# Layer 2 attention in units of four heads, with the first batch's units placed among the first layer's segments

## The chip, the cores and the metric

The kernel runs on one core of one Trainium2 chip. The metric is the device time of one execution in microseconds, as the median of several runs. All times below come from the runs and from one profiled execution of the kernel before.

## The reference

The input x has 4 batches of 2048 tokens with 256 features, in float32. Two layers follow each other, each of the form x = x + s * silu(g), where s is an attention and g a feed-forward network, both on a layer norm of x.

```python
# layer 1
xn = layernorm(x)
s = dilated_attention(xn)   # 16 heads of 16; segments of 512 queries, every 8th key: 64 keys;
                            # maximum over blocks of 64 queries; then @ Wout.T
g = xn_rounded_to_fp8 @ w8.T + bias
x = x + s * silu(g)
# layer 2
xn = layernorm(x)
q, k, v = xn @ wq + bq, xn @ wk + bk, xn @ wv + bv      # rotary positions on q and k
att = softmax(causal(q @ k.T / 4))                      # 16 heads of 16, 2048 x 2048 each
s = (att @ v) @ wo + bo
g = mixture_of_experts(xn)  # 8 experts, top 2 of a softmax, capacity 2048 slots each,
                            # relu(x @ w1 + b1) @ w2 + b2, hidden 1024
x = x + s * silu(g)
```

The two parts of layer 2 that cost most are the causal attention (4 batches x 16 heads, head size 16) and the experts (16384 slots in blocks of 512).

## The kernel before, in words

Everything is float32. The order of the instructions on TensorE (PE), VectorE (DVE), ScalarE (ACT) and GpSimd (POOL) is the order of the program: the blocks under `manual_schedule` leave nothing to a scheduler. Transfers are issued from the queue of SyncE (SP), indirect ones from POOL's.

**First layer** (L133 to L380). 16 segments of 512 tokens run in a software pipeline of 8 steps per segment. `segment` writes functions into a plan by step (`at`, L175), and the plan is then run in order of steps. A segment loads x (L182), normalizes it, transposes it (`turn_x`, L199), rounds to fp8 (`to_fp8`, L213), projects q, k and v, makes scores against 64 keys (`scores0`, L273), takes block maxima and exponentials (`weigh`, L285), multiplies with the values (`values`, L297), transposes (`turn_y`), projects (`outputs`, L320), gates (`gate`), stores x1, normalizes again, and stores this norm to DRAM as `xn_d` together with the router's logits (`route`, L350). In PSUM two pair tiles of two banks each (`sc`, L52) and four tiles of one bank (`mm`, L53) are used. Most SBUF tiles have two buffers, x six, the weights w nine.

**Routing** (L398 to L552). When all segments are done, softmax, top 2 and the places in the experts' slots are computed, mostly on DVE. This is one block with nothing beside it.

**Second layer.** PSUM is divided anew: three pair tiles `sp` (L562) and two single tiles `so` (L563). For each batch, two phases follow each other in the loop L1059 to L1076:

- `maxima` (L691). For each query block qb of 512, each row group r of 128 queries and each group g of four heads, scores of 128 queries against up to 512 keys are made by four matmuls that work on 32 rows of the array each (`scores`, L677). DVE reduces full key blocks straight from PSUM (L720). The diagonal block is copied by ACT (L723), masked on POOL (L731) and reduced (L740). The negated maxima are transposed (`spread`, L751) and written as an extra row into q, so that later scores come out with the maximum subtracted.
- `attend` (L765). For each qb, g and tile kt of 128 keys, the transposed scores are made, ACT takes exponentials from PSUM (L826), POOL masks the diagonal (L831), and two items later the values are multiplied (L846). Per qb and g the result is copied (L852), transposed and divided (`heads_out`, L803), and per qb projected (`out_rows`, L771).

Beside these run side generators, which `along` (L1034) advances by costs written by hand. `project` (L594) makes q, k and v of a batch from `xn_d`; its results stay in a ring of five SBUF blocks. `experts` (L878) runs two experts' blocks beside each batch's maxima. `finish` (L956) combines the experts' outputs with s and x1 beside the last batch's `attend`. So at any time maxima (DVE) or exponentials (ACT) run, not both.

Of the kernel before, what the change touches and what calls it, by code (L numbers as in the profile page):

```python
# [18 lines left out]
P = 128  # L19
# [24 lines left out]
def d2_kernel(ctx: ExitStack, tc: tile.TileContext, t: dict):  # L44
# [6 lines left out]
    first = ExitStack()  # L51
    ps_sc = first.enter_context(tc.tile_pool(name="ps_sc", bufs=2, space=PSUM))  # L52
    ps_mm = first.enter_context(tc.tile_pool(name="ps_mm", bufs=4, space=PSUM))  # L53

    def sc_tile():
        return ps_sc.tile([P, 2, 512], F32, tag="sc", name="sc")

    def mm_tile():
        return ps_mm.tile([P, 512], F32, tag="mm", name="mm")
# [6 lines left out]
    xn_d = dram.tile([B * M + 1, D], F32, tag="xn_d", name="xn_d")  # L66
    s_d = dram.tile([B * M, D], F32, tag="s_d", name="s_d")
# [7 lines left out]
    def rows(d, n):  # L75
# [11 lines left out]
    early = ExitStack()  # L87
    logits = early.enter_context(tc.tile_pool(name="early", bufs=1)).tile(
        [P, NT, E], F32, tag="logits", name="logits"
    )  # L90
# [28 lines left out]
    def transpose2(out, in_):  # L119

        tp = mm_tile()
        for c in range(2):
            nc.tensor.transpose(tp[:, c * P : (c + 1) * P], in_[:, c * P : (c + 1) * P], ident)
        nc.scalar.copy(out, tp[:, : 2 * P].rearrange("p (c t) -> p c t", c=2))

    def silu(pool, zh):

        th = pool.tile([P, D], F32, tag="se", name="se")
        nc.scalar.activation(th, zh, AF.Tanh)
        nc.vector.scalar_tensor_tensor(zh, th, 1.0, zh, ALU.add, ALU.mult)  # L130


    with ExitStack() as l0:  # L133
        w0 = l0.enter_context(tc.tile_pool(name="w0", bufs=1))
        p2 = l0.enter_context(tc.tile_pool(name="l0p2", bufs=2))
        small = l0.enter_context(tc.tile_pool(name="l0small", bufs=4))
# [27 lines left out]
        for i in range(3):  # L164
            v_ = w0.tile([P, 8, 2, HD + 1], F32, tag=f"vbd{i}", name=f"vbd{i}")
            nc.vector.tensor_copy(v_[:, :, :, HD], bc(dmask[:, None, :], [P, 8, 2]))
            vbds.append(v_)
# [7 lines left out]
        def at(step, f, *args):  # L175
            plan.setdefault(step, []).append((f, args))

        def segment(g):
# [3 lines left out]
            def load():  # L182
                v["x"] = x = p2.tile([P, SPT, D], F32, tag="x", name="x", bufs=6)
                nc.sync.dma_start(out=x, in_=rows(x_d, g))
# [7 lines left out]
            def norm(tag):  # L192
                v[tag] = xn = p2.tile([P, SPT, D], F32, tag=tag, name=tag)
# [5 lines left out]
            def turn_x(c):  # L199
                if c == 0:  # L200
                    v["xnT"] = p2.tile([P, 2, SEG], F32, tag="xnT", name="xnT")

                    v["xdil"] = p2.tile([P, 2, 2, KN], F32, tag="xdil", name="xdil")
                tp = mm_tile()
                for a in range(SPT):
                    nc.tensor.transpose(
                        tp[:, a * P : (a + 1) * P], v["xn"][:, a, c * P : (c + 1) * P], ident
                    )
                nc.scalar.copy(v["xnT"][:, c, :], tp)
                for u in range(2):  # L210
                    nc.gpsimd.tensor_copy(v["xdil"][:, c, u, :], v["xnT"][:, c, ::DIL])

            def to_fp8(half):  # L213


                if half == 0:
                    v["xq"] = xq = p2.tile([P, 2, SEG], F32, tag="xq", name="xq", bufs=3)
# [4 lines left out]
                mag = p2.tile([P, 2, SEG], F32, tag="mag", name="mag")  # L222
# [7 lines left out]
            def q_proj(ec):  # L230
                if ec == 0:
                    v["qT"] = p2.tile([P, 2, SEG], F32, tag="qT", name="qT")
                pq = mm_tile()
                for c in range(2):
                    nc.tensor.matmul(  # L235
# [897 lines left out]
```

## Time and profile before

| | us |
|---|---|
| median of 3 runs | 4508.95 (4506.05 to 4519.44) |
| profiled execution | 4471.85 |
| its span, first to last instruction | 4470.1 |
| PE busy | 4090.9 |
| DVE busy | 2447.8 |
| ACT busy | 1664.1 |
| POOL busy | 851.3 |

The span is some 1.75 us shorter than the profiled execution's own time, and that execution was 0.8% faster than the median of the runs. A page of the profile gives busy time by engine, a division of the span in 40 slices (each 112 us), the chain of work that ended last, and groups of instructions by line. In the groups the name before `<-` is the tile written, the names after it are those read. A float32 matmul shows as two instructions, a transpose as one. "Busy" of PE includes time in which a matmul only waits in the array's pipeline or runs at a lower granted clock.

In this span the first layer takes the first 620 us, the routing about 100, and then each batch some 450 us of maxima with experts and some 450 us of exponentials. The first batch's maxima take longer (756 to 1333 us), and the last batch's exponentials, with the final combination, 394.

### The profile page before, as it was taken

Reading aid. Unit: us, or ns where it says so; the run is one execution under the profiler, and the core shown is the slowest. Engines: PE = TensorE matmul, PEld = TensorE weight load, DVE = VectorE, ACT = ScalarE, POOL = GpSimd, SP = SyncE. Lnnn points to the kernel's source line nnn. Section 1 sums busy time; section 2 is a strip of 40 time slices with the busy share of each in tenths; the row PEclk is TensorE's granted clock in tenths of the full one; section 3 lists DMA queues with packets and bytes.
Section 4 is the critical chain, followed back from the end, with each engine's and each line's share of the span. In section 5 each row is a group of like instructions: output and inputs, shape, how many; then the busy total and the mean of one; then the engine's idle time right before and its main releaser. Section 6 shows DMA issues by size and latency. Waiting matters only on the chain.

```text
span 4470.1 us, 57281 instructions
## 1 busy us (share of the span) xinstructions
PE 4090.9 (92%) x23560; PEld 1930.8 (43%) x23560; DVE 2447.8 (55%) x3622; ACT 1664.1 (37%) x2548; POOL 851.3 (19%) x1067
## 2 busy tenths in 40 slices
PE   7898966789999998899999998999999989999998
PEld 4666654344443333444433334444333344443333
DVE  7777777667761122777812226777312257775334
ACT  2333310111116664222156652211566522114775
POOL 3333323101100012111100012110000121112444
PEclk8888777699999998899999998999999989999999
DMA  2111000000100001001000001010000010102422
GB/s 77 43 43 43 29 33 25 10 15 24 38 20 6 10 6 41 20 20 39 15 10 6 10 14 46 16 40 18 6 10 6 15 36 20 39 20 74 128 94 75
DMA packets 111240, 138.48 MB, mean 31 GB/s; under 512 B 11393, under 2 KB 99842, under 8 KB 110978
## 3 DMA queue, kind: packets, MB, share of 16 engines
q1 hardware_dynamic: 95922, 98.22, 6.7%
q0 software_dynamic: 12288, 33.57, 2.4%
q8 instruction: 185, 3.03, 0.3%
q10 hardware_dynamic: 2768, 3.02, 0.2%
q14 instruction: 77, 0.63, 0.0%
HBM read 86.03 MB, written 48.24 MB: 30 GB/s over the span
## 4 chain that ended last, share of the span: by engine, by line
PE 79%; DVE 15%; issue 2%; DMA 1%; ACT 1%; POOL 1%; POOLq 0%; ACTq 0%; SPq 0%; DVEq 0%
PE sp L683 29%; PE so L846 11%; PE so L926 10%; PE so L941 9%; DVE mp L720 4%; PE so L626 3%; PE mm L300 2%; PE so L666 2%; PE mm L323 1%; PE so L635 1%; PE so L787 1%; PE sc L278 1%; DVE at_row L538 1%; PE mm L328 1%; PE mm L235 1%
## 5 line engine op out<-in xcount | busy, mean ns | idle before, releaser
L826 ACT ACTIVATE pt<-sp 128x1024 f32<-128x1024 f32 (+3 forms) x1280 | 1076.8, 893 | 577.2 <-PE sp L683 541.6
L720 DVE TENSOR_REDUCE mp<-sp 128x2 f32<-128x1024 f32 x768 | 904.5, 1220 | 317.7 <-PE sp L683 314.9
L683 PE MATMUL sp<-kT,qT 32*128 32x512 f32 (+3 forms) x5120 | 785.1, 615 | 63.9 <-DVE mp L725 25.9
L683 PE MATMUL sp<-qT,kT 32*128 32x512 f32 (+3 forms) x5120 | 783.4, 583 | 13.6 <-ACT pt L826 13.5
L846 PE MATMUL so<-pt,va 128*32 128x512 f32 (+3 forms) x5120 | 604.6, 545 | 10.9 <-POOL pt L831 10.9
L723 ACT COPY dg<-sp 128x256 f32<-128x256 f32 x512 | 165.3, 375 | 962.6 <-PE sp L683 899.1
L926 PE MATMUL so<-xTe,w 128*128 128x512 f32 x1024 | 515.9, 628 | 4.3 <-ACT xTe L918 2.0
L941 PE MATMUL so<-w,hT 128*128 128x256 f32 x2048 | 506.6, 392 | 0.3 <-DVE ot L947 0.3
L731 POOL TENSOR_SCALAR_AFFINE_SELECT dg<-dg 128x512 f32<-128x512 f32 x256 | 163.2, 640 | 1578.7 <-ACT dg L723 1578.6
L683 PEld LDWEIGHTS sp<-kT,qT 32*128 32x128 f32 x5120 | 270.6, 197 | 444.6 <-issue 146.0
L683 PEld LDWEIGHTS sp<-qT,kT 32*128 32x128 f32 x5120 | 282.9, 184 | 407.6 <-issue 254.0
L941 PEld LDWEIGHTS so<-w,hT 128*128 128x128 f32 x2048 | 374.0, 191 | 193.2 <-issue 143.5
L831 POOL TENSOR_SCALAR_AFFINE_SELECT pt<-pt 128x512 f32<-128x512 f32 x256 | 171.7, 672 | 1310.4 <-PE sp L683 677.1
L930 ACT ACTIVATE hT<-so,b 128x512 f32<-128x512 f32 x256 | 176.0, 687 | 572.5 <-PE so L926 572.5
L725 DVE TENSOR_REDUCE mp<-sp 128x2 f32<-128x256 f32 (+2 forms) x384 | 247.5, 687 | 145.2 <-ACT dg L723 144.2
L926 PEld LDWEIGHTS so<-xTe,w 128*128 128x128 f32 x1024 | 178.1, 193 | 283.1 <-issue 199.6
L846 PEld LDWEIGHTS so<-pt,va 128*32 128x32 f32 x5120 | 101.5, 108 | 418.9 <-issue 345.0
L852 DVE COPY avs<-so 128x512 f32<-128x512 f32 x64 | 44.2, 691 | 360.7 <-PE so L846 360.7
L740 DVE TENSOR_REDUCE mp<-dg 128x8 f32<-128x1024 f32 x128 | 155.0, 1211 | 31.5 <-POOL dg L731 31.5
L626 PE MATMUL so<-wqk,xT 128*128 128x512 f32 x256 | 139.9, 672 | 23.8 <-DVE xT L622 9.5
L294 ACT ACTIVATE w<-w 128x1024 f32<-128x1024 f32 x64 | 67.7, 1057 | 241.4 <-DVE w L290 241.4
L300 PE MATMUL mm<-vbd,w 128*128 128x34 f32 x1024 | 128.7, 283 | 21.5 <-DVE vbd L267 21.5
(165 smaller groups left out, 3514.9 us busy)
## 6 DMA issues: line engine op xcount, KB each, us to landing
w<-in_w_dram SPq DMA_DIRECT2D x16, 1024.0 KB, 6.3
eout<-ot SPq DMA_DIRECT2D x32, 512.0 KB, 2.9
x<-in_x_dram SPq DMA_DIRECT2D x16, 512.0 KB, 5.9
x_d<-x SPq DMA_DIRECT2D x16, 512.0 KB, 2.9
xn_d<-x1n SPq DMA_DIRECT2D x16, 512.0 KB, 3.2
xn<-xn_d SPq DMA_DIRECT2D x16, 512.0 KB
fx<-x_d SPq DMA_DIRECT2D x16, 512.0 KB, 5.5
out_dram<-fz SPq DMA_DIRECT2D x16, 512.0 KB, 4.1
```

The costliest lines, as they stand in the source:

```text
L300: nc.tensor.matmul(av[:, j * 34 : (j + 1) * 34], lhsT=v["w", j // 2][:, j % 2, a * P : (a + 1) * P], rhs=vbds[g % 3][:, j, :, :].rearrange ...
L626: nc.tensor.matmul(pqk, lhsT=xT[:, c, :], rhs=wqk[:, c, :], start=(c == 0), stop=(c == 1))
L683: nc.tensor.matmul(pairs[j // 2][:, j % 2, :w], lhsT=lhsT[r0 : r0 + 32], rhs=rhs[r0 : r0 + 32], start=True, stop=True,)
L720: nc.vector.tensor_reduce(mp[:, h0 : h0 + 2, kc], sp, AX.X, ALU.max)
L723: nc.scalar.copy(dg[:, d0 : d0 + 2, :], sp[:, :, r * P : w])
L725: nc.vector.tensor_reduce(mp[:, h0 : h0 + 2, qb + 1], sp[:, :, : r * P], AX.X, ALU.max)
L826: nc.scalar.activation(pt[:, 2 * p : 2 * p + 2, c0:], sp[:, :, : SEG - c0], AF.Exp, scale=SCALE)
L831: nc.gpsimd.affine_select(out=pt[:, :, c0 : c0 + P], in_=pt[:, :, c0 : c0 + P], compare_op=ALU.is_ge, fill=0.0, base=0, pattern=[[0, 4], [ ...
L846: nc.tensor.matmul(av[32 * j : 32 * j + 32, c0:], lhsT=va[:, kt % 4, h0 : h0 + 32], rhs=pt[:, j, c0:], start=(kt == 0), stop=last,)
L926: nc.tensor.matmul(ph, lhsT=w1[:, c, hc * P : (hc + 1) * P], rhs=xT[:, c, :], start=(c == 0), stop=(c == 1),)
L930: nc.scalar.activation(hT[:, hc, :], ph, AF.Relu, bias=b1[:, hc : hc + 1])
L941: nc.tensor.matmul(po[:, u * D : (u + 1) * D], lhsT=hT[:, hc, a * P : (a + 1) * P], rhs=w2[:, hc, :], start=(hc == 0), stop=(hc == 7),)
```

## The change

The second layer's attention is cut into 16 units: unit n is the group g = n % 4 of four heads of batch n // 4. The pieces of the change:

- PSUM is divided once for the whole program: three pair tiles `sp`, one bank `av` for the value sums, and one bank `mm` for everything else. The first layer uses the same pair tiles for its transposes, q, scores, values and outputs, and `mm` for the rest. Its SBUF pool has one buffer for most tiles (x four, w six, two sets of values).
- `project` reads the transposed norm, which the first layer now stores to DRAM too (`xT_ds`), so it makes no transposes of x. It writes q, k and v to DRAM. `load_unit` loads q, k and v of a unit into a set of SBUF tiles. There is one set during the first layer, two afterwards.
- `maxima(n)` and `attend(n)` work on a unit. The values are multiplied one item after their exponentials (two before). Heads are stored to DRAM (`y_ds`); `out_project` reads them back and projects.
- `attention` yields the order: while there is one set, maxima of a unit, then its exponentials, then the next unit. With two sets, each item of `attend(n)` is followed by one step of `maxima(n + 1)`, three items late.
- The first layer is a generator, and so is the routing. During the first layer, from 30% of its hand-written cost on, `project` and then the units of the first batch (`EARLY = 4`) are advanced. Routing, all experts and the final combination run beside the paired units. In the experts' second product each tile of 128 slots has its own bank use (two shared one before).

```diff
-    first = ExitStack()
-    ps_sc = first.enter_context(tc.tile_pool(name="ps_sc", bufs=2, space=PSUM))
-    ps_mm = first.enter_context(tc.tile_pool(name="ps_mm", bufs=4, space=PSUM))
+    ps_s = ctx.enter_context(tc.tile_pool(name="ps_s", bufs=3, space=PSUM))
+    ps_v = ctx.enter_context(tc.tile_pool(name="ps_v", bufs=1, space=PSUM))
+    ps_m = ctx.enter_context(tc.tile_pool(name="ps_m", bufs=1, space=PSUM))
...
+    def load_unit(n):
+        b, g = n // 4, n % 4
+        held[n] = sets[(sets.index(held[n - 1]) + 1) % len(sets) if n else 0]
+        qT, kT, va = held[n]
+        nc.sync.dma_start(out=qT, in_=q_ds[b][g])
+        nc.sync.dma_start(out=kT, in_=k_ds[b][g])
+        nc.sync.dma_start(
+            out=va[:, :, :VW],
+            in_=v_ds[b][:, g * VW : (g + 1) * VW].rearrange("(i p) c -> p i c", p=P),
+        )
...
+        yield from start(0)
+        for _ in maxima(0):
+            yield MX_T, 1
+            turn()
+        for n in range(NU):
+            two = len(sets) == 2 and n + 1 < NU
+            if two:
+                yield from start(n + 1)
+            a = attend(n)
+            m = maxima(n + 1) if two else iter(())
+            a_on, step = True, 0
+            while True:
+                if a_on:
+                    a_on = next(a, None) is not None
+                    if a_on:
+                        yield S_T, 0
+                        next(a)
+                m_on = step < LEAD or next(m, None) is not None
+                if not (a_on or (two and m_on)):
+                    break
+                yield (AV_T if a_on else 0.0) + (MX_T if two and step >= LEAD else 0.0), 1
+                turn()
+                step += 1
+            units_done[0] += 1
+            if not two and n + 1 < NU:
+                yield from start(n + 1)
+                for _ in maxima(n + 1):
+                    yield MX_T, 1
+                    turn()
...
+        with ExitStack() as l0:
+            went = 0.0
+            for cost in first_layer(l0):
+                went += cost
+                if EARLY:
+                    f = max(0.0, (went / L0_T - 0.3) / 0.7)
+                    if f:
+                        prj.until(prj_share())
+                    while f and 0 in ready and not att.over and att.went < f * EARLY * UNIT_T:
+                        if units_done[0] == EARLY - 1 and 1 not in ready:
+                            prj.step()
+                            break
+                        att_step([])
+                elif went / L0_T > 0.35:
+                    prj.until(PRJ_T * min(1.0, (went / L0_T - 0.35) / 0.55))
+        ub = ctx.enter_context(tc.tile_pool(name="ub", bufs=1))
+        sets.append(unit_set(ub, "b"))
+        done = {}
+        opr = Side(out_project(ub, done))
+        with ExitStack() as rt:
+            rou = Side(routing(rt))
+            t0 = att.went
+            while not rou.over:
+                rou.burst = 3
+                att_step([
+                    (prj, 0, prj_share), (opr, 0, lambda: 1e9),
+                    (rou, 0, lambda: (att.went - t0) * 2.2), (rou, 1, lambda: (att.went - t0) * 2.2),
+                ])
+        with ExitStack() as xs:
+            ep = xs.enter_context(tc.tile_pool(name="ex", bufs=2))
+            exp = Side(experts(ep, 0, E), 2)
+            exp.step()
+            t0 = att.went
+            last = 13.7 * UNIT_T
+            while not exp.over:
+                att_step([
+                    (prj, 0, prj_share), (opr, 0, lambda: 1e9),
+                    (exp, 1, lambda: EXP_T * (att.went - t0 - 2.0) / (last - t0)),
+                ])
+        fp = ctx.enter_context(tc.tile_pool(name="fp", bufs=2))
+        fin = Side(finish(fp, done))
+        t0 = att.went
+        while not att.over:
+            att_step([
+                (opr, 0, lambda: 1e9),
+                (fin, 1, lambda: NT * (att.went - t0) / (16 * UNIT_T - t0)),
+                (fin, 0, lambda: NT * (att.went - t0) / (16 * UNIT_T - t0)),
+            ])
```

A `Side` runs one step of its generator per call of `until` (experts two, routing three) as long as its cost is below the share given. `att_step` advances the attention by one yield; kind 0 stands between scores and values, kind 1 after the maxima's scores, and kind 2 means that the unit's batch has not been projected yet. `prj_share` is PRJ_T x (1.2 + att.went / (4 UNIT_T)), UNIT_T is 120, L0_T 443.

## The prediction

> **What bounds the kernel now.** I read the page's parts 1, 2 and 4 first: who is busy, when, and on which chain.
>
> ```profile
> PE 4090.9 (92%) x23560; PEld 1930.8 (43%) x23560; DVE 2447.8 (55%) x3622; ACT 1664.1 (37%) x2548; POOL 851.3 (19%) x1067
> ...
> PE   7898966789999998899999998999999989999998
> DVE  7777777667761122777812226777312257775334
> ACT  2333310111116664222156652211566522114775
> PEclk8888777699999998899999998999999989999999
> ...
> PE 79%; DVE 15%; issue 2%; DMA 1%; ACT 1%; POOL 1%; POOLq 0%; ACTq 0%; SPq 0%; DVEq 0%
> ```
>
> TensorE is busy for 92% and carries 79% of the chain that ended last. DVE and ACT alternate: where the maxima run DVE is at 7 or 8 tenths and ACT at 1 or 2; where the exponentials run it is the other way round. The granted clock is 0.8 in the first layer, 0.6 after it, 1.0 later. Next, sums by stage (columns: window, its length, busy us of PE, PEld, DVE, ACT, POOL, clock, DMA):
>
> ```profile
> 20.00:620.00 600.00, 526.31 (x2742) 394.15 (x2741) 446.87 (x1009) 186.82 (x397) 220.17 (x251) 0.82 0.12 39
> 620.00:721.00 101.00, 46.17 (x268) 38.18 (x268) 91.36 (x176) 1.99 (x4) 37.19 (x27) 0.79 0.05 13
> ...
> 850.00:880.00 30.00, 24.69 (x86) 10.40 (x88) 18.78 (x24) 3.82 (x11) 3.18 (x5) 0.50 0.00 0
> ...
> 1790.00:2240.00 450.00, 434.00 (x2074) 205.94 (x2071) 341.17 (x366) 88.52 (x191) 62.84 (x84) 0.97 0.07 23
> 2240.00:2700.00 460.00, 429.74 (x3056) 158.68 (x3054) 104.65 (x192) 275.55 (x339) 50.35 (x76) 0.97 0.05 16
> 4076.00:4470.00 394.00, 366.34 (x2721) 123.33 (x2720) 146.84 (x241) 282.65 (x336) 172.71 (x192) 0.98 0.33 104
> ```
>
> 20 to 620 is the first layer (16 segments, 36.4 us each by the spacing of its repeated rows), 620 to 721 the routing, 1790 to 2240 maxima with experts, 2240 to 2700 exponentials, 4076 to 4470 exponentials with the final combination. 850 to 880 is a rare stretch in which maxima run with almost nothing beside them: half clock, PE "busy" 82% only because every instruction is twice as long. Three timelines give prices. Maxima alone:
>
> ```profile
> 854.00 2.36 DVE L720 TENSOR_REDUCE mp<-sp 128x2 f32<-128x1024 f32 x2 [1.84 <-PE sp L683]
> 855.28 4.89 PE L683 MATMUL sp<-kT,qT 32*128 32x256 f32 x16 [1.33 <-DVE mp L720]
> ...
> 860.21 2.36 DVE L720 TENSOR_REDUCE mp<-sp 128x2 f32<-128x1024 f32 x2 [1.84 <-PE sp L683]
> 861.49 4.23 PE L683 MATMUL sp<-kT,qT 32*128 32x256 f32 x16 [1.33 <-DVE mp L720]
> ```
>
> One short diagonal score group plus one full group take 5.56 to 6.21 us (starts of 855.28, 861.49): PE waits for the first DVE reduce, DVE then waits for PE. Exponentials:
>
> ```profile
> 1404.54 1.06 PE L846 MATMUL so<-pt,va 128*32 128x512 f32 x8
> 1404.71 1.94 ACT L826 ACTIVATE pt<-sp 128x1024 f32<-128x1024 f32 x2 [0.37 <-PE sp L683]
> 1405.53 1.38 PE L683 MATMUL sp<-qT,kT 32*128 32x512 f32 x8
> 1406.85 1.06 PE L846 MATMUL so<-pt,va 128*32 128x512 f32 x8
> ```
>
> One full item (scores L683, values L846) takes 2.31 us from start to start, of which ACT works 1.94; scores wait until ACT frees a pair tile. Maxima with experts:
>
> ```profile
> 1157.29 1.14 PE L683 MATMUL sp<-kT,qT 32*128 32x512 f32 x8
> ...
> 1158.36 1.98 PE L926 MATMUL so<-xTe,w 128*128 128x512 f32 x4
> ...
> 1160.28 1.14 PE L683 MATMUL sp<-kT,qT 32*128 32x512 f32 x8
> ```
>
> A full maxima group and four expert passes (1.82 us) take 2.99 us, so PE has no gap worth naming there.
>
> **What the Trainium skill says.** "TensorE: Matmul & The Clock Gate", Part 1: the clock has two levels, half and full; idle or thinly used windows of about 3.4 us put it back to half. The trace agrees: 0.50 in 850 to 880, 1.00 in dense stretches. "Perfetto Trace Analysis", Optimization Strategy: where the contended engine changes between regimes, interleaving the regimes may help. Here DVE's and ACT's stages are such regimes, but TensorE is near 95% busy in both. The same page, Optimizing Tensor Performance, Matmuls: independent groups should rotate through PSUM banks so that evacuation overlaps the next group. No trace of the kernel before shows a single rotating bank; its side work has two or four.
>
> **The change, part by part.** Prices at full clock from the rows above and the chain: a 512-column pass 0.456 us (8 in 3.65), 256 columns 0.228 (16 in 3.65), a transpose 0.15 (4 in 0.60), a full score group 1.05, a full value group 1.0. A unit (four heads, 24 full and 16 diagonal groups) is then 37 us of PE for maxima, 37 for scores, 36 for values. The work is the old one: dropped are only 128 transposes of project (19 us), added 192 tiny ones for the maxima (29 us). The rest is order, so I take the changed program's order of TensorE's instructions, cut it where its character changes, and price each piece.
>
> (1) The first 11 or so segments' PE work with the whole project of batch 0: 316 + 63 = 379 us. Before, the first layer did 16 x 28 = 448 us of such work in 620, a ratio of 0.72: 525 us. But three pair tiles now serve what two plus four banks served, side results have one bank, most SBUF tiles one buffer; PE then waits for DVE's 28 us per segment instead of overlapping. Bounds 500 and 660; I take 570.
>
> (2) What the diff hides: project advances one step per step of the first layer, some 92 steps, so batch 0 is ready only after about the twelfth segment. Then the loop catches up in one go: maxima 0, exponentials 0, maxima 1, exponentials 1, maxima 2, with nothing beside them. Lone maxima, half clock: 4 r-rows at qb 0 of 2.75 us (16 steps in 44 us at 756 to 800), then 4 x 6.2, 4 x (6.2 + 3.4), 4 x (6.2 + 6.8), with 3.4 = 2.07 PE + 1.22 reduce + hand-overs: 126 us. At full clock DVE would bound it at 88. Exponentials: 24 x 2.31 and diagonals, 92 to 100 us (457 us for four units before, less about 85 for project and projections; the lag falls from two items to one, so a diagonal waits for POOL's 0.67 us); I take 95. The single operand set cannot be loaded early; 2 MB at this row's rate:
>
> ```profile
> w<-in_w_dram SPq DMA_DIRECT2D x16, 1024.0 KB, 6.3
> ```
>
> is 13 us per change of unit. Sum: 3 x 126 + 2 x 95 + 2 x 13 = 594 (bounds 480, 630).
>
> (3) Exponentials of unit 2 with nearly two segments: PE 152 us at the density of 0.85: 180. (4) The loop waits for batch 1, so the layer's tail runs with project alone: 114 / 0.74 = 155. (5) Maxima 3, exponentials 3, alone: 126 + 95 + 9 of leftovers = 230. (6) Routing beside most of maxima 4: DVE has 98 us of routing (91 before, and 16 adds of 0.29) and 60 of maxima; PE's half clock and order leave gaps: 190 (bounds 158, 225).
>
> (7) The paired stage: exponentials n with maxima n+1, all experts, projects and projections: PE 2211 us over 375 steps. At the density of the row 1790 to 2240 without its start (0.96): 2303. On top, the single bank: in the order some 230 side tiles follow another with less PE work between than the evacuation needs (0.42 to 0.69 us plus hand-overs); their shortfalls sum to 165 us, 75 of them Relu after Relu, 0.86 each. 44 maxima groups are followed directly by scores, which need the tile of the first reduce: 1.28 us each, 56. Values to maxima, waiting for the first exponential: 30. Half of 251 may overlap: 125. 2430 (bounds 2300, 2560). Here is the gain: before, scores and values took 2.31 per item, here about 2.1 with the maxima free of DVE's pace.
>
> (8) The end: 74 paired steps without experts. PE 207, 59 direct hand-overs x 1.28 and 74 x 0.15: 294; lone last unit 37 x 2.4 = 90; projections and a last store, reload and combine 45. 430 (370, 540 at half clock).
>
> Sum: 570 + 594 + 180 + 155 + 230 + 190 + 2430 + 430 = 4779, against the span of 4470: +309. The profiled execution took 4471.85, the median of the runs 4508.95, 0.83% above. 4779 x 1.0083 = 4818; I give 4815. Costed at nothing: the detour of q, k, v, x and y through DRAM adds some 110 MB to 138, but DMA is busy for 2 to 14% in nearly all stages, and in the paired stage a unit's loads have three steps (12 to 18 us) before the first maxima need them. SP's queue is passed too: a unit's loads wait there for the last value group of the set's former unit, and behind them stand segment loads and stores; in (2) nothing of these is due soon. If that cover is gone, a late load stalls PE at each of 11 paired starts, 5 us each, 55. The added bank waits of (7) stand in PE's queue: behind a waiting side tile stand the next scores, behind those ACT's exponentials, which is why they count in full unless ACT or DVE is still at work.
>
> **Rivals.** *Faster.* TensorE keeps full clock through the lone maxima (DVE's 88 us each) and the buffers suffice: pieces 520, 480, 165, 130, 195, 160, 2300, 400 = 4350, x 1.0083 = 4386. It is decided by the clock in (2): what speaks for it is that attention before held 1.00; against it, 850 to 880 at 0.50 for the same loop. Four half-clock maxima alone are 150 us; the point is where all the other pieces meet their lower bounds too. 0.10. *Within 0.3%*: the two cancel, 0.02. *Slower still.* The three shared pair tiles lock PE and DVE step by step in the first layer and at the end: (1) 660, (2) 630, (4) 180, (7) 2560, (8) 540, the rest as above: 5170, 5213. For it: PE and DVE are both at 75 to 88% there now. 0.15. *It doesn't interleave*: by the order it largely doesn't in the first layer; that is part of the forecast.
>
> **Numbers.** Forecast 0.73, much slower 0.15, no change 0.02, faster 0.10; a measurement tells 0.3% from no change. Slower 0.88, same 0.02, faster 0.10. The range 4560 to 5050 leaves out most of the faster rival and the worst of the slow one.
>
> **What would show it.** Between roughly 570 and 1170 us slices with PE at 5 to 8 tenths, clock 5 to 7, DVE and ACT alternating; then ACT and DVE both at 4 to 5 with PE 9 from 2000 on; PE waits on ACT Relu and on DVE's reduces. Wrong if the clock there is near 1.0, if the first 12 segments end before 520, or if the paired stage needs under 2300.

## The result, and the profile after

The changed kernel takes 5195.9 us (median of 4 runs, 5186.4 to 5204.2), the kernel before beside it 4514.2: ratio 1.151, 95% interval 1.147 to 1.154. The forecast was 4815, 4560 to 5050; the direction is right, the size is not, and the time lies above the range. The profiled execution's span is 5184.7 us. Since the medians of the kernel before differ by about 1% between the chips (4475 to 4523 us), what follows compares ratios to the kernel before on the same chip, or spans and stages of traces.

The page of the changed kernel, parts 1, 2 and 4, with the lines that answer to those shown of before (a slice is now 130 us):

```profile
PE 4416.3 (85%) x23624; PEld 2067.0 (40%) x23624; DVE 2415.4 (47%) x3477; ACT 1676.7 (32%) x2436; POOL 835.4 (16%) x968
...
PE   5777778888766877899999989999999999998887
DVE  5655561625344629444444434444443333336652
...
PEclk7676768586876587999999999999999999999888
...
PE 70%; DVE 17%; issue 7%; ACT 5%; DMA 1%; POOL 1%; another core or an unknown queue 0%; SPq 0%; POOLq 0%; ACTq 0%; DVEq 0%
```

From slice 16 on the picture is the one that was meant: DVE and ACT work beside a PE at 9 tenths and full clock. The loss lies in the sixteen slices ahead of it and in the last four: PE at 5 to 8 tenths, with a clock of 0.5 to 0.8 in the early ones. PE's busy time grew by 325 us, for nearly the same arithmetic: at a lower clock the same matmul is listed for longer (128x512 of L625: 592 ns in the median, up to 1222). The eight pieces of the forecast's sum, cut in the trace where the kernel's activity changes (columns: window, its length, busy us of PE, PEld, DVE, ACT, POOL, clock, DMA share, GB/s):

```profile
0.00:683.00 683.00, 474.92 (x2168) 337.05 (x2168) 391.75 (x757) 127.23 (x169) 156.68 (x131) 0.75 0.19 62
683.00:1230.00 547.00, 463.71 (x2314) 165.77 (x2316) 254.34 (x273) 171.98 (x267) 50.98 (x80) 0.71 0.04 12
1230.00:1462.00 232.00, 184.80 (x1088) 91.50 (x1084) 82.96 (x159) 88.65 (x111) 36.97 (x36) 0.83 0.13 45
1462.00:1697.00 235.00, 159.94 (x684) 109.64 (x684) 114.51 (x217) 26.99 (x46) 33.20 (x25) 0.72 0.20 63
1697.00:1946.00 249.00, 199.33 (x1018) 71.30 (x1020) 113.09 (x145) 81.93 (x119) 24.25 (x40) 0.71 0.10 33
1946.00:2076.00 130.00, 100.52 (x480) 59.83 (x476) 121.79 (x221) 9.49 (x27) 41.10 (x31) 0.73 0.01 2
2076.00:4653.00 2577.00, 2391.82 (x13288) 1080.46 (x13288) 1044.01 (x1325) 942.45 (x1393) 313.91 (x427) 0.99 0.15 46
4653.00:5184.00 531.00, 441.22 (x2592) 151.43 (x2588) 292.99 (x386) 227.98 (x306) 178.29 (x200) 0.87 0.28 89
```

| piece | forecast | measured | difference |
|---|---|---|---|
| 1, first segments with project 0 | 570 | 683 | +113 |
| 2, the lone units | 594 | 547 | -47 |
| 3, exponentials with segments | 180 | 232 | +52 |
| 4, the layer's tail with project 1 | 155 | 235 | +80 |
| 5, unit 3 alone | 230 | 249 | +19 |
| 6, routing with maxima 4 | 190 | 130 | -60 |
| 7, the paired stage | 2430 | 2577 | +147 |
| 8, the end | 430 | 531 | +101 |

The lone units, the forecast's main argument, cost what it said. Wrong are the first layer's pieces (1, 3 and 4, together +245), the paired stage and the end. The rival "slower still" had 660, 630, 180, 2560 and 540 for pieces 1, 2, 4, 7 and 8; it came within 25 us on three of these five, and had been given 0.15. The experiments ask which causes are behind these numbers.

### The profile page after: what moved, and what is told of

It reads as the page before. It is cut to its first block, busy times and chain, and to the rows that moved or that the text cites. A ratio compares the mean times of both kernels' runs of the same rounds, so it can differ in the third digit from the quotient of the medians.

```text
span 5184.7 us, 57621 instructions
## 1 busy us (share of the span) xinstructions
PE 4416.3 (85%) x23624; PEld 2067.0 (40%) x23624; DVE 2415.4 (47%) x3477; ACT 1676.7 (32%) x2436; POOL 835.4 (16%) x968
## 4 chain that ended last, share of the span: by engine, by line
PE 70%; DVE 17%; issue 7%; ACT 5%; DMA 1%; POOL 1%; another core or an unknown queue 0%; SPq 0%; POOLq 0%; ACTq 0%; DVEq 0%
PE sp L291 26%; PE av L416 10%; PE mm L1033 9%; PE mm L1046 9%; DVE mp L325 4%; PE mm L210 3%; ACT hT L1037 2%; PE mm L255 1%; ACT pt L397 1%; PE mm L220 1%; PE sp L685 1%; PE mm L508 1%; PE sp L717 1%; DVE cm L670 1%; DVE w L672 1%
## 5 line engine op out<-in xcount | busy, mean ns | idle before, releaser
L291 PE MATMUL sp<-kTa,qTa 32*128 32x512 f32 (+3 forms) x3200 | 668.1, 726 | 92.8 <-DVE mp L325 56.7
L1033 PE MATMUL mm<-xTe,w 128*128 128x512 f32 x1024 | 509.1, 620 | 65.6 <-ACT hT L1037 58.4
L291 PE MATMUL sp<-qTa,kTa 32*128 32x512 f32 (+3 forms) x3200 | 518.3, 601 | 53.5 <-DVE mp L325 30.3
L1046 PE MATMUL mm<-w,hT 128*128 128x256 f32 x2048 | 481.6, 389 | 6.2 <-ACT hT L1037 5.4
L291 PEld LDWEIGHTS sp<-kTa,qTa 32*128 32x128 f32 x3200 | 250.4, 225 | 492.0 <-DVE mp L325 214.7
L1046 PEld LDWEIGHTS mm<-w,hT 128*128 128x128 f32 x2048 | 382.4, 192 | 138.0 <-issue 70.0
L416 PE MATMUL av<-pt,vaa 128*32 128x512 f32 (+3 forms) x3200 | 391.4, 562 | 29.8 <-POOL pt L402 25.7
L291 PE MATMUL sp<-qTb,kTb 32*128 32x512 f32 (+3 forms) x1920 | 313.7, 591 | 33.7 <-DVE mp L325 23.9
L291 PE MATMUL sp<-kTb,qTb 32*128 32x512 f32 (+3 forms) x1920 | 315.9, 614 | 12.2 <-DVE mp L329 5.3
L416 PE MATMUL av<-pt,vab 128*32 128x512 f32 (+3 forms) x1920 | 234.2, 561 | 2.1 <-POOL pt L402 2.0
```

The source lines that it names most:

```text
L291: nc.tensor.matmul(pairs[j // 2][:, j % 2, :w], lhsT=lhsT[r0 : r0 + 32], rhs=rhs[r0 : r0 + 32], start=True, stop=True,)
L416: nc.tensor.matmul(av[32 * j : 32 * j + 32, c0:], lhsT=va[:, kt, h0 : h0 + 32], rhs=ppt[:, j, c0:], start=(kt == 0), stop=last,)
L1033: nc.tensor.matmul(ph, lhsT=w1[:, c, hc * P : (hc + 1) * P], rhs=xT[:, c, :], start=(c == 0), stop=(c == 1),)
L1046: nc.tensor.matmul(po[:, :D], lhsT=hT[:, hc, a * P : (a + 1) * P], rhs=w2[:, hc, :], start=(hc == 0), stop=(hc == 7),)
```

## The experiments

Four theories came up for the first layer: one side bank `mm` (A), single SBUF buffers (B), an order that makes TensorE wait for DVE (C), and three pair tiles `sp` for everything (D).

### The early units

```diff
-    EARLY = 4
+    EARLY = 0          # e1_early0
+    EARLY = 2          # e13_early2
```

> The changed kernel with EARLY = 0: no unit of attention runs in the first layer, only the first batch's projection; all 16 units are then paired. Theory A (lone units are what the early placement costs): the first layer with one projection takes about 920 us (510 us of PE work at the 379/683 of the changed kernel's first piece), routing with maxima 0 130, the paired stage 2728/0.858 = 3180, the end 530: span near 4760, some 420 below the changed kernel and still above the kernel before. Rival B (the units themselves, their shared PSUM and the detour through DRAM are the cost, the early placement is neutral): within 60 us of 5185.

> The changed kernel with EARLY = 2: two units of the first batch among the first layer instead of four. Theory: the cost is per lone unit (about 215 us alone against about 155 beside the paired stage's other work) and from the experts packed into fewer paired units; half of the 400 us between none and four goes: 4950 to 5050. Rival, a fixed cost of coupling the first layer with any attention: over 5080.

Measured: EARLY = 0 4793.0 us, ratio 1.062 (1.058 to 1.066); EARLY = 2 4954.7 us, 1.096 (1.091 to 1.101). Placing the units early costs 9% of the 15%, and two units cost 39% of what four do. By the first and last of the experts' second products (L1046), experts begin at 1134, 1490 and 2144 us with none, two and four early units, and run for 3105, 2920 and 2508 us. So a unit early adds 178 us (two) or 252 us (four) ahead of the experts and takes 92 or 149 us from the paired stage: a net loss of about 85 to 105 us each. Both runs came out where they were expected. What remains without any early unit, 6%, is the new design itself.

Is it the clock? The lone full maxima steps in the changed kernel's timeline:

```profile
986.64 2.78 PE L291 MATMUL sp<-kTa,qTa 32*128 32x512 f32 x8 [0.20 <-DVE mp L325]
988.76 2.36 DVE L325 TENSOR_REDUCE mp<-sp 128x2 f32<-128x1024 f32 x2 [1.05 <-PE sp L291]
990.04 1.65 PE L291 MATMUL sp<-kTa,qTa 32*128 32x384 f32 x4 [0.63 <-DVE mp L325]
```

A step takes 3.40 us (986.64 to 990.04), DVE working 2.36 of it and waiting 1.05 for PE, as forecast. The next run adds useless work to it:

```diff
+    def filler():
+        tp = mm_tile()
+        for _ in range(2):
+            nc.tensor.matmul(tp, lhsT=ident, rhs=wqk[:, 0, :], start=True, stop=True)
...
         for _ in maxima(0):
             yield MX_T, 1
+            filler()
             turn()
...
                 for _ in maxima(n + 1):
                     yield MX_T, 1
+                    filler()
                     turn()
```

> The changed kernel with two useless 512-column matmuls after each lone maxima step (units 0 to 3), whose result is not read: more work on PE. Theory A (the lone maxima are slow because thin use keeps PE at half clock): with 1.8 us more work per step the clock returns to full, a lone maxima unit falls from 114 us towards 95 to 100, the span by 40 to 80. Rival B (the lone maxima are bound by DVE and by hand-overs whatever the clock): each step gets longer by what the fillers take beyond DVE's work, span up by 50 to 200.

Measured: 5234.7 us, 1.160 (1.155 to 1.165).

```profile
986.21 1.14 PE L291 MATMUL sp<-kTa,qTa 32*128 32x512 f32 x8
987.28 1.98 PE L437 MATMUL mm<-wqk,ident 128*128 128x512 f32 x4
...
989.19 0.31 PEld L291 LDWEIGHTS sp<-kTa,qTa 32*128 32x128 f32 x8 [0.76 <-DVE mp L325]
989.19 1.14 PE L291 MATMUL sp<-kTa,qTa 32*128 32x512 f32 x8
```

With 1.8 us of useless matmuls in it a full step takes 2.98 us, less than without, and the clock in the three lone maxima is 1.00 where it was 0.56 to 0.58. So here the thin use of the array goes with the half clock, and more use lifts it. No idle window of the 3.4 us that the forecast cites was needed: in the changed kernel TensorE is never idle for more than 1.7 us within these units. But a whole lone maxima unit takes about as long as before, 116 to 119 us with the fillers against 114 to 117: what the full steps gain, the short diagonal steps lose again. Both forecasts are missed, that of a faster unit and that of longer steps. The run as a whole is some 0.9% slower, and the trace has this loss in a place that the forecast did not name: unit 4's maxima, which run beside the routing, get the fillers too and take 222 us instead of 173. So the half clock is real, and lifting it with work that nobody needs wins nothing.

Could the units be spread finely among the segments?

```diff
         with ExitStack() as l0:
             went = 0.0
+            prj.burst = 4
...
+        prj.burst = 1
```

> The changed kernel with up to four projection steps, not one, per step of the first layer, so that batch 0 is ready near segment 9 instead of 12; by the order 55 lone maxima steps and 40 lone exponential items remain in one block instead of 120 and 81, the others stand among the first layer's segments. Theory A (lone units are the cost, interleaving helps): 150 to 300 us faster than the changed kernel, span 4890 to 5035. Rival B (the in-order queues couple the layer and the attention so that interleaving gains nothing): within 60 us of 5185.

Measured: 5248.9 us, 1.162 (1.157 to 1.167), about 1% more than the changed kernel and a little outside both ranges, although in TensorE's order some 60% of the early units' steps now stand among segments (some 15% in the changed kernel). The half of the theory that called the missing interleaving the loss falls. In this order a segment and a unit gain nothing from each other.

### The paired stage

```diff
                         next(a)
+                        yield 0.0, 3
...
-            exp = Side(experts(ep, 0, E), 2)
+            exp = Side(experts(ep, 0, E), 1)
...
+                    (exp, 3, lambda: EXP_T * (att.went - t0 - 2.0) / (last - t0) - 1.0),
```

> The changed kernel with the experts' steps no longer two in a row after the maxima: at most one there and one between values and maxima, so that a Relu never has its next user right behind it; by the order the 75 Relu-to-matmul pairs on the one bank go away. Theory A (the single side bank's waits count in full): the paired stage gets 65 to 100 us shorter, span 5085 to 5120. Rival B (PE waits elsewhere as soon as it does not wait here, for a pair tile or an exponential): within 25 us of 5185.

Measured: 5112.9 us, 1.134 (1.129 to 1.138), some 80 us less. TensorE's waits between 2076 and 4653 us in the changed kernel (columns: who waited for whom, us, times, longest):

```profile
PE mm L1033 <- ACT hT L1037: 58.4, 75, 0.8
...
PE mm L1022 <- ACT xTe L1025: 18.0, 25, 1.5
```

Each of these 75 expert products that directly follow another finds the only side bank still under ACT's Relu, 0.8 us each. Set one at a time with values or scores between, this row is gone from the list of TensorE's waits, and the experts last 2419 us instead of 2508. All of TensorE's idle time before matmuls into the side bank falls from 155 to 81 us in this stage, and the run gets some 80 us shorter: the bank's waits count in full.

### The first layer

The runs from here on have no early units, but for e16_after_spread; e15_before_piled changes the kernel before. Without early units the first layer with project 0 takes 906 us (e1_early0); before, the layer alone took 620. One or two banks, one or two buffers, an earlier norm:

```diff
     def mm_tile():
-        return ps_m.tile([P, 512], F32, tag="mm", name="mm")
+        flip[0] += 1                                   # e5_banks
+        if two_banks[0] and flip[0] % 2:               # until the routing starts
+            return ps_v.tile([P, 512], F32, tag="av", name="av")
+        return ps_m.tile([P, 512], F32, tag="mm", name="mm")
...
-        p1 = l0.enter_context(tc.tile_pool(name="l0p", bufs=1))
+        p1 = l0.enter_context(tc.tile_pool(name="l0p", bufs=2))   # e6_bufs
...
-            do(t0 - 9, 0, stats, "0")
-            do(t0 - 8, 0, norm, "xn")
+            do(t0 - 10, 0, stats, "0")                 # e7_norm
+            do(t0 - 9, 0, norm, "xn")
```

> No early units, and the side results rotate through two PSUM banks (the idle value bank and the side bank) until the second layer's attention starts. Without it the first layer with project 0 takes 906 us of a span of 4777. Theory A, the one side bank stretches the first layer: PE's short waits there for the evacuation of the bank (0.5 to 1.2 us each, some 70 to 110 us in all) go, 4670 to 4710. Theory B, the single SBUF buffers: within 20 us of 4777. Theory C, the coarse order (DVE's norm of the next segment lies behind two statistics and a double block of weights, and TensorE's transposes wait for it, 126 us in 13 waits): PE only waits longer there, 4740 to 4775.

> No early units, and two SBUF buffers instead of one for all single-buffered tiles of the first layer (the attention's own pool is taken from the first layer's space for that). Theory B, the single buffers stretch the first layer: 60 us or more off the span of 4777. Theories A (bank) and C (order): within 20 us of 4777.

> No early units, and the first norm's statistics and the norm itself one step earlier in the first layer's plan (t0 - 10 and t0 - 9), nothing else. The order on TensorE is as before. Theory C, the coarse order: the 126 us of TensorE's transposes waiting for the norm shrink to under 30, 4650 to 4700. Theories A and B: within 30 us of 4777.

Measured: e5_banks 4694.8 us, 1.048 (1.043 to 1.053), first layer 810; e6_bufs 4792.1, 1.068 (1.063 to 1.074), first layer 906; e7_norm 4820.7, 1.076 (1.071 to 1.082), first layer 944. A holds: 96 us of the first layer in the trace, some 60 us by the ratios (1.062 to 1.048). B falls. C failed in this form: the earlier norm made the layer longer. Yet with two banks TensorE waits even more before the transposes of x:

```profile
PE sp L600 <- DVE xn L126: 180.7, 16, 25.8
```

The next two moved the norm with the banks doubled, and then took the transposes off the pair tiles:

```diff
             def turn_x():
-                tp = pair_tile()
-                for c in range(2):
+                for c in range(2):                     # e11_side_turn, e12_best
+                    tp = mm_tile()
...
-                nc.scalar.copy(xnT, tp)
+                    nc.scalar.copy(xnT[:, c, :], tp)
```

> No early units, two side banks in the first layer, and the norm one step earlier. With the banks alone the first layer with project 0 took 810 us of a span of 4692. Theory C (the order, hidden behind the bank until now): the 181 us of waiting for the norm go, 4560 to 4620. Theory D (three shared pair tiles: the transposes need the tile that the weights' subtraction releases, so the wait only changes its name): 4670 to 4720, and TensorE's transposes wait for the subtraction instead.

> As the run with two side banks and the earlier norm, and the transposes of x go through the two side banks instead of a pair tile. Theory D (pair tiles and order together): TensorE's waits before the transposes fall under 40 us, the first layer with project 0 to 690 to 740 us, the whole 4580 to 4630. Theory that the rest of the first layer is bound elsewhere (DVE's outputs, clock): 4660 to 4710.

> As the run before it, and the experts' pieces are split over both halves of a paired step, one at a time, so that two uses of the side bank do not follow each other. With early units this took 83 us off; without them the experts are less dense, and TensorE's waits for the side bank after Relu and the copies are some 80 us: 20 to 70 us less than the run before it, if the first layer gains as theory D says 4530 to 4600, still slower than the kernel before.

Measured: e10_banks_norm 4746.9 us, 1.050 (1.045 to 1.055); e11_side_turn 4757.5, 1.052 (1.047 to 1.057); e12_best, with the experts one at a time, 4743.7, 1.049 (1.044 to 1.054), 14 us less than e11_side_turn where 20 to 70 were expected. By the ratios none differs from e5_banks; in the traces the first layer is longer than its 810 us, 859, 873 and 871, as it was longer with the earlier norm in e7_norm. In e10_banks_norm the wait has only another name:

```profile
PE sp L600 <- DVE w L678: 170.3, 14, 15.6
```

It was put down to the norm, then to the release of a pair tile; through side banks it was the norm again and copies on DVE. What does not change is that DVE comes late. One segment in the timeline of e1_early0 shows why:

```profile
409.95 0.75 DVE L608 TENSOR_SCALAR xq<-xnT,inv_isc 128x1024 f32<-128x1024 f32 x1
410.73 1.64 DVE L609 TENSOR_SCALAR xq<-xq 128x1024 f32<-128x1024 f32 x1
...
417.08 1.09 PE L255 MATMUL mm<-ident,qa 128*128 128x128 f32 x4
417.28 0.41 DVE L112 BATCH_NORM_STATS2 bn<-x 128x6 f32<-128x256 f32 x1
...
424.49 1.37 DVE L120 TENSOR_SCALAR xn<-x,mean,rstd 128x256 f32<-128x256 f32 x4
425.04 1.35 PE L594 MATMUL sp<-ident,xn 128*128 128x128 f32 x4 [6.87 <-DVE xn L120]
```

DVE has worked without a pause since 404.3. From 409.95 on it does the fp8 rounding, both statistics, two weights, then the norm, ending at 425.9, 16 us later; call this DVE's pile. All of it stands in plan steps 6, 7 and 0 of a segment. TensorE has 8 us of work for that time and then waits 6.87. Later in the segment the roles change: DVE waits 133 us in this layer for TensorE's `outputs` (L723). Moving one piece inside the pile leaves the rest of it there. So the pile was taken apart:

```diff
-            do(t0 - 9, 0, stats, "0")
+            do(t0 - 11, 0, stats, "0")
...
-            do(t0 - 2, 0, to_fp8, 0)
-            do(t0 - 1, 0, to_fp8, 1)
+            do(t0 - 6, 0, to_fp8, 0)
+            do(t0 - 5, 0, to_fp8, 1)
...
-            do(t0 + 16, 0, stats, "1")
+            do(t0 + 17, 0, stats, "1")
```

with a third buffer for `xq`. e16_after_spread is the changed kernel, with its four early units, and this edit alone; e17_spread_between is e14_spread with the experts one at a time; e15_before_piled makes a pile in the kernel before:

```diff
-            at(t0 - 10, stats, "0")
+            at(t0 - 9, stats, "0")
...
-            at(t0 - 5, to_fp8, 0)
-            at(t0 - 4, to_fp8, 1)
+            at(t0 - 2, to_fp8, 0)
+            at(t0 - 1, to_fp8, 1)
...
-                at(t0 + 2 * i, weigh, i)
+                at(t0 + 2 * (i - i % 2), weigh, i)
```

> No early units and two side banks (1.048 times before, first layer with project 0 in 810 us), and DVE's pile taken apart: fp8 rounding at t0 - 6 and t0 - 5 instead of t0 - 2 and t0 - 1 (a third buffer for it), the first statistics at t0 - 11, the second at t0 + 17. Theory, the pile is what TensorE's transposes wait for: their wait falls from 181 us under 70, the first layer to 680 to 740 us, the ratio to 1.020 to 1.038. Rival, the first layer is bound by the chain of a segment through all engines: wait and ratio stay (1.042 to 1.052).

> The changed kernel (1.151 times before) with DVE's pile in the first layer taken apart as above, nothing else. Theory of the pile: the 93 us that the transposes wait for the norm before 683 us mostly go, and some of the tail's; ratio 1.125 to 1.143. Rival: 1.147 to 1.155; the one side bank takes the wait over.

> As e14_spread, and the experts' pieces one at a time in both halves of a paired step. If all adds up: 5 to 15 us less than e14_spread, ratio 1.018 to 1.036, the best version of the changed design here, slower than before all the same.

> The kernel before with DVE's work piled up as in the changed one: fp8 rounding at t0 - 2 and t0 - 1, the first statistics at t0 - 9, the weights of both tiles of a score group in one step; banks and buffers as before. Theory of the pile: TensorE waits for the norm 3 to 8 us per segment, the first layer grows from 620 to 670 to 750 us, ratio 1.011 to 1.029. Rival: within 0.5% of before.

Measured: e14_spread 4619.2 us, 1.023 (1.019 to 1.028), first layer 733 instead of 810; e16_after_spread 5107.9, 1.132 (1.128 to 1.136), its first maxima at 635 us instead of 686; e17_spread_between 4587.6, 1.017 (1.014 to 1.021), 32 us less than e14_spread where 5 to 15 were expected. The wait itself, in e14_spread:

```profile
PE sp L600 <- DVE xn L126: 59.9, 12, 25.8
```

181 us became 60, as expected, and in the changed kernel itself the edit takes the ratio from 1.151 to 1.132. The pile is a cause. e15_before_piled misses its forecast, and its rival holds: 4535.0 us, 1.004 (1.002 to 1.007). There the wait for the norm grew from 7.4 to 65.9 us, but the layer only from 620 to 646. So a pile makes the wait in the kernel before too, and more than half of it is won back. Why is not shown. The kernel before has four side banks and score tiles of their own, and the pile made in it is the smaller one: up to the end of the norm DVE works without a pause for 11.2 us there in the median, against 16.5 in e1_early0, 10.1 in e14_spread, 6.8 in e16_after_spread and 3.8 in the kernel before.

### The end

```diff
-        last = 13.7 * UNIT_T
+        last = 14.7 * UNIT_T
```

> No early units, and the experts are spread to 14.7 units instead of 13.7, so that about 40 of the 74 uncovered pairs at the end get experts beside them. Theory of the end (pairs without experts run at DVE's and ACT's hand-overs, PE 83% busy there at a clock of 0.87): 20 to 45 us less than 4777. Rival, the last combination with its gathers needs that time: equal or up to 60 us more.

Measured: 4775.7 us, 1.067 (1.061 to 1.072), no gain over 1.062, as the rival had it. The experts end at 4405 instead of 4239 us, the end is shorter by about as much, the sum stays. A paired step there, in the changed kernel:

```profile
4716.86 1.07 PE L416 MATMUL av<-pt,vaa 128*32 128x512 f32 x8
4717.86 1.38 PE L291 MATMUL sp<-kTb,qTb 32*128 32x512 f32 x8
4719.03 1.13 PE L291 MATMUL sp<-qTa,kTa 32*128 32x512 f32 x4
4720.57 1.13 PE L291 MATMUL sp<-qTa,kTa 32*128 32x512 f32 x4 [0.41 <-DVE mp L325]
4721.63 1.06 PE L416 MATMUL av<-pt,vaa 128*32 128x512 f32 x8
```

4.77 us from values to values, where the rows have 3.1 us of work at the prices of the forecast. The maxima's scores (kTb,qTb) come in one piece. The second half of the exponentials' scores (qTa,kTa at 4720.57) waits until a reduce on DVE frees a pair tile, so that each half runs alone. The last two runs alternate the tiles between the engines, with scores cut into halves of two heads:

```diff
+    def half(w, lhsT, rhs, p):
+        sp = pair_tile()
+        for j in (2 * p, 2 * p + 1):
...
+                got = next(a, None) if a_on else None
+                a_on = got is not None
+                m_on = step < LEAD or next(m, None) is not None
+                if a_on and got == 2:
+                    next(a)
+                if two and m_on and step >= LEAD:
+                    next(m)
                 if a_on:
...
+                    yield S_T, 0
+                    yield 0.0, 3
+                    next(a)
```

This is e18_alternate: both generators give their halves in turn, and the values follow. In e19_split the values stand between the two halves of each.

> As e17_spread_between (1.0174 times before; its last 435 us are the end), and in a paired step the pair tiles alternate between the engines: exponentials, maxima, exponentials, maxima, where before both exponential tiles came ahead of both maxima tiles; the values follow after them. The work is the same. Theory, the lock-step over three pair tiles sets the 4.77 us of an uncovered paired step: these steps take 3.2 to 3.8 us, the end 330 to 380 us, the ratio 0.990 to 1.006. Rival, the clock or the last combination sets it: end and ratio stay within 20 us (1.013 to 1.022).

> As e17_spread_between (1.0174 times before), and a paired step goes: first exponential tile with first maxima tile, values, second exponential tile with second maxima tile, so that four matmuls on four row groups still stand together, and both tiles of an engine are a half step apart. Lone steps as in e17_spread_between. Theory A, the loss of the alternating run (1.110) was the lost overlap of row groups alone: the ratio falls back under 1.02; with the shorter lock-step of an uncovered paired step (3.6 to 4.2 us instead of 4.77) 1.000 to 1.012. Rival, alternating the tiles couples ACT and DVE more tightly and costs in the whole paired stage: 1.03 to 1.09.

Measured: e18_alternate 4979.1 us, 1.110 (1.107 to 1.113); e19_split 4587.9 us, 1.023 (1.021 to 1.025), both from 1.017; neither lies in one of its forecast's ranges. In e18_alternate two matmuls of a half stand alone:

```profile
4711.81 1.02 PE L307 MATMUL sp<-qTa,kTa 32*128 32x512 f32 x4
4713.14 1.13 PE L307 MATMUL sp<-kTb,qTb 32*128 32x512 f32 x4 [0.31 <-ACT pt L418]
```

Two take 1.02 us where four together take 1.05. The Trainium skill, "TensorEngine Tiling (Array Packing)", Key Properties, says that different tiles of the array work in parallel; here that means a group of four costs no more than two, and a half alone pays for all. In a paired step of e18_alternate two of the four halves run together and two alone, so a step loses one group: at 1.05 us for 555 paired steps (15 pairs of units, 37 steps each) up to 580 us, less where the diagonal makes groups short, and some 400 were lost. e19_split keeps four row groups together in most of the stage with experts and gets this back. In the end without experts alternating does shorten a step, to 4.36 us in e18_alternate and 4.30 in e19_split in the median, though halves still run alone there; from the last expert product on e19_split takes 519 us instead of 546. But its stage with experts takes 3109 us instead of 3082, and the sum is what it was.

## Why the forecast was wrong, step by step

*The lone units, (2) and (5): right.* "Lone maxima, half clock", 126 us with steps of 3.4: 114 to 117 us with steps of 3.40, clock 0.50 in the long runs of full steps. That the first layer hides nothing of them is right too. (6) was too dear by 60 us: DVE had 122 us of work in it, not the 158 that were counted.

*The first layer, (1), (3) and (4): the failed step.* It is "Before, the first layer did 16 x 28 = 448 us of such work in 620, a ratio of 0.72: 525 us", with 45 us on top for banks and buffers. It priced the new layer by the density of the old one and compared totals ("PE then waits for DVE's 28 us per segment"), without laying the two engines' orders side by side. The runs show two causes in its place. DVE's pile of 16 us, an effect of moved plan steps that the forecast did not name: about 85 us in the changed kernel (1.151 to 1.132), some 50 of them in piece 1. And the one side bank: 60 to 96 us without early units; in the changed kernel it could not be tried, since the value bank is in use there. If it costs as much there, some 65 to 100 of the 245 us remain open. The values and outputs now come in double blocks, and DVE waits 133 us for the outputs (17 in the kernel before); no run took these blocks apart. The forecast's worry about "one buffer" was without ground (e6_bufs).

*The paired stage, (7): a size.* "Half of 251 may overlap: 125." The waits for the bank did not overlap: the forecast had 75 of them after a Relu at 0.86 us, some 65 us, and halved them with the rest; the trace has exactly 75, with 58 us, and taking these and some others away gave some 80 us. Behind a waiting side tile stand the next scores and behind those the exponentials, as its last sentence said; by that argument it should have kept the full 251, which gives 2303 + 251 = 2554 against the 2577 measured. That this sum comes so near is in part luck. TensorE idles for 186 us in the stage: 155 before side-bank matmuls, near the 165 that the forecast counted, but only 31 for the other 86. In return its busy time is 2392 us, not the 2211 that were priced. That the bank's waits count in full agrees with the advice of the Trainium skill, "Perfetto Trace Analysis", Optimizing Tensor Performance, Matmuls, that independent groups rotate through PSUM banks so that one is emptied while the next is filled; this case has a price for not doing so, 0.8 us per use.

*The end, (8): open.* 377 us of paired steps, where 294 were priced, and 154 for the last unit with the rest, where 135 were. The lock-step of 4.77 us is in the trace, and another order of the tiles took 0.4 to 0.5 us of it away. But neither this nor experts beside it made the whole shorter, and halves of a group still ran alone, so how much the pair tiles cost stays open. The last combination's work on DVE, which stands between the reduces, and the clock of 0.87 are candidates that no run separated.

*The rival "slower still"* had nearly the right numbers for three pieces, and part of the mechanism. "Three shared pair tiles lock PE and DVE" is not what the first layer showed: its transposes without a pair tile gained nothing (e11_side_turn). What deserved more than 0.15 was that nothing in the profile had tried the new order of the first layer, with one bank, so its bound belonged near the forecast, not at the edge. The signs of being wrong that the forecast named (a clock near 1.0, first segments before 520, a paired stage under 2300) all looked to the fast side, and none of them came.

*The sign.* It was right, and the forecast's reason is the larger part of it: the early units' loss is 9 of the 15%. But the kernel is slower without any early unit too, which the forecast did not say. The best version here, with none of them early, the pile apart, two banks in the first layer and experts one at a time, is still 1.7% slower than the kernel before (1.014 to 1.021). Cut at the end of the first layer, its trace has 733 + 3852 us and that of the kernel before 620 + 3850. So what is left of the loss stands in the first layer, which has the first batch's projection in it (63 us at the forecast's price), and behind it the pairing, with the routing beside it, gains nothing that rises above the 1% between chips. A likely reason, which no run separates: TensorE was busy for 96 and 93% of the two old phases (434 of 450 and 430 of 460 us), so pairing them had little to win.

## What to carry to other kernels

When work is moved in a hand-written order, lay the queues of two engines side by side over one period, and add up how long one works without a pause while the other has nothing left; totals per period don't show it. If the name of a wait changes with each edit and its length stays, look for what stands ahead of the released instruction on its queue. And count a wait for a single rotating bank in full when the next critical work stands behind it on the same queue.

## What the runs showed of the hardware

In the pile the same DVE instruction on 128x1024 took 1.64 us (L609 and L613, median of 16) where the kernel before needs 0.69 for it. At 410.11 to 413.5 us POOL works on `gate` (1.71 and 1.59 us) beside them. In the traces of the changed kernel and of e1_early0 the first two of the 16, which have no `gate` beside them, take 0.69 us, the other 14 take 1.64. In e15_before_piled, where `gate` works on 256 columns instead of 512, L219 takes 1.10 us; with the rounding moved away, in e14_spread, the median is 0.69 again. L608, which starts just before the same POOL instruction and overlaps it for 0.6 us, stays at 0.75. The Trainium skill's "GPSIMD Engine Reference", Key points, says that POOL shares its SBUF interfaces with DVE, with contention for DVE instructions in a 2-port mode or with two SBUF inputs. L609 has one input, and its mode no run shows; that the two get in each other's way, the traces do show, at a factor of 2.4 and 1.9 us per segment. So part of the pile was made by what had been put beside it.
